# States beside heads: sums with the identity, 1/A moved to VectorE, six states of a batch added in pairs, and the first slot's order changed

## The chip, the cores and the metric

The kernel runs on one core of one Trainium2 chip. The metric is the device time of one execution in microseconds; the figure for a kernel is the median of its runs. Engines are named as in the profile: PE is TensorE (matrix products), PEld its weight loads, DVE is VectorE, ACT is ScalarE, POOL is GpSimd, SP the engine that issues most of the DMAs.

## What is computed

A decoder of three stages over 8 batches of 256 tokens with 128 features, all in float32. Stage one is a state-space block with 256 channels and 16 states, stage two a cross attention with 16 heads to a context of 256 tokens, stage three six layers of windowed attention and feed-forward. Each stage ends in a residual and a layer norm. The change lies in stages one and two. The state-space block, cut to what matters:

```python
X_main = silu(causal_conv4(Xn @ W_up1.T) + conv_b)          # [b, l, 256]
pp = X_main @ W_ll.T + b_ll
delta = softplus(pp[..., :256]); Bm = pp[..., 256:272]; Cm = pp[..., 272:]
A = -exp(A_log)                                              # [256, 16]
A_bar = exp(delta * A)
B_bar = (A_bar - 1) / (delta * A) * (delta * Bm)             # = (A_bar - 1) / A * Bm
H_t = A_bar_t * H_{t-1} + X_main_t * B_bar_t                 # a scan over 256 tokens
Y_t = sum over n of C_t[n] * H_t[:, n]
out = X + (Y * silu(Xn @ W_up2.T)) @ W_down.T + b_down
```

The factor 1/A belongs to a channel and a state and not to a time, so it can be applied before the scan or after it.

## The kernel before

**Tiles.** Channels lie on the partitions, as two halves `h` of 128; time (256) lies along the free axis, so a batch's work on one state is a tile of 128 x 512. Batches go in four pairs `p`; the convolution, the time steps `dt`, the gate and the B and C rows are made once a pair, for 512 tokens.

**Slots and steps.** The loop at the end of stage one calls `step(u, i)` for each batch u and state i (n in the code); k = 16u + i. The 16 steps of one batch are called slot u here. While slot u runs the states of batch u, batch u-1 goes through its cross attention: eight pairs of heads j = i - 6, in steps 6 to 13 and a little after. Slot 0 has no heads.

**Order.** A manual schedule holds PE, ACT, DVE and POOL to the order in which the program issues instructions, so what stands behind a waiting instruction on its engine waits too. Extra work is put into the steps by `at(u, i, when, ...)`, where `when` is E, M or L: early, in the middle or late in the step. A step runs in this order: the row fetch for k+4 (DMA on SP); `scores2` of head pair j (PE); `add_up` (PE); `denominators` (ACT) and `weight_sums` (POOL) of earlier heads; `scan(k)`; `outputs` (DVE); the E list; `decay_of(k+1)` (ACT); `clipped` (DVE, then ACT); `values2` (PE); the M list; `spread_b(k+2)`; the L list.

**One state.** `spread_b(k)` makes wz = x * B on DVE (L604, from `xm_ps` in PSUM and the row B; L608 for the first two states) and dw, its difference in time, on POOL (L613). `decay_of` makes ab = A_bar on ACT in a PSUM bank, two halves (recorded at L98); slots 1 to 7 have one bank for it, slot 0 two in turn. `scan` runs two scans on DVE (L631), m = (dw + m) * ab, and multiplies by the row C on POOL (mc, L633). `add_up` sums mc over the states in the PSUM bank `y`, as a matrix product per half whose weights are a diagonal of 1/A (`by_a`, L644); `decay` builds the 32 diagonals at the start on POOL (L408). `start_y` opens `y` with a product of 512 columns and the identity (L671). A float32 product runs as two passes, so the trace shows two matmuls, and two weight loads, for each in the code.

**Around it.** At the end of batch v's states `gated` (L676), `down` (L249, `dn_ps`) and `down_leave` (L254, `rr`) lead to the layer norm of v in steps 1 to 3 of the next slot: `ln_square` on ACT (L214), `ln_var` on PE (L218), `ln_roots` on ACT, `ln_latent` on DVE (L231, `la`). `queries` (L302, `q_ps`) and `queries_leave` follow in steps 4 to 11, `vals` (L287) and `keys` (L272) beside them. `prepare(p)` lays the making of pair p into the slots before it: statistics, `turn_x`, `copy_x` (L456), `norm_x`, `shifted` (L483), `conv` (L489, 16 passes of 512 columns into the two-bank tile `big`), `conv_tanh`, `conv_plus` (L504), `conv_out` (L508), `bc_product` and `bc_store` (L522, then by DMA to DRAM and back as rows), `gate_products` (L565), `dt_product` (L537) and `dt_parts`, `dt_log`, `dt_sum`. For p = 0 this is done ahead of slot 0, for p = 1 in slots 0 and 1, for p = 2 and 3 the convolution falls in slots 2 and 4 and `dt` in slots 3 and 5. `context_of(u)` norms and turns the context of batch u. `centre_rows` subtracts row means from `w_dn` and `wo` on ACT (L875).

## Time and profile before

| | us |
|---|---|
| median of 3 runs | 2152.8 (2150.98 to 2156.37) |
| profiled execution: its time / span from first to last instruction | 2151.4 / 2149.6 |
| first scan of slots 0 to 7 starts at | 31.8, 85.3, 149.8, 215.7, 282.7, 347.7, 413.8, 471.8 |
| yg of the last batch (end of the states) | 530.2 |
| busy, whole span: PE / DVE / POOL / ACT | 2035 / 1706 / 1649 / 1481 |

The slots take 53.5, 64.5, 65.9, 67.0, 65.0, 66.1, 58.0 and some 55 us; from about 546 us on the rest of the span is stage three, with PE busy in nine tenths and more of nearly every slice. A line of the profile names source line, engine, operation, the tiles out<-in, shape and count. A matmul's duration includes a tail that overlaps the next, so what a set of matmuls costs is read from start to start, or from the chain of waits, which counts only the time until the next link. Mean durations that matter here: L604 (wz, DVE, 128x512) 0.68 us, L613 (dw, POOL) 1.04, L633 (mc, POOL) 1.27, L631 (one half's scan, DVE) 0.67, ab (one half, ACT) 0.48, one pass of L644 (256 columns) 0.38 and of L671 (512 columns) 0.59.

### The profile page before, as it was taken

The numbers are of one execution on the slowest core, as the hardware profiler recorded it, in microseconds if no ns is written. First come the engines' busy times: TensorE is split into PE (matmuls) and PEld (weight loads), VectorE is DVE, ScalarE is ACT, GpSimd is POOL, SyncE is SP. The second block draws the span as 40 slices with busy tenths as digits, with TensorE's granted clock in tenths as the row PEclk, the third lists the DMA queues.
The fourth block names the chain that finished last, engine by engine and source line by source line (L and its number), as shares of the span: only waits on it lengthen the run. The fifth ranks groups of instructions, "written<-read, shape, count | busy, mean of one in ns | idle before, by whom it ended". The sixth has DMA issues, their size and how long they took to land.

```text
span 2149.6 us, 78066 instructions
## 1 busy us (share of the span) xinstructions
PE 2035.1 (95%) x32880; PEld 1376.6 (64%) x32880; DVE 1705.5 (79%) x2535; ACT 1481.2 (69%) x2657; POOL 1648.8 (77%) x1453
## 2 busy tenths in 40 slices
PE   6899999899989999999999999999999999999985
PEld 3555556566457776666766667676666767666663
DVE  5767767687589888888888888888888888888752
ACT  5767767666667777776676777677777767767654
POOL 4677767778599888888888888888888888888740
PEclk8999999999999999999999999999999999999997
DMA  4323323232244444343434344443443444333330
GB/s 120 94 63 71 62 68 73 64 74 65 79 74 70 71 95 72 70 77 68 92 71 78 69 75 86 74 78 66 88 74 70 78 71 82 66 66 66 61 57 10
DMA packets 455195, 156.13 MB, mean 73 GB/s; under 512 B 402046, under 2 KB 451068, under 8 KB 454716
## 3 DMA queue, kind: packets, MB, share of 16 engines
q1 hardware_dynamic: 454364, 150.76, 36.5%
q8 instruction: 258, 4.23, 0.9%
q14 instruction: 93, 0.76, 0.1%
q10 hardware_dynamic: 480, 0.38, 0.1%
HBM read 55.33 MB, written 1.31 MB: 26 GB/s over the span
## 4 chain that ended last, share of the span: by engine, by line
PE 77%; ACT 10%; DVE 10%; issue 2%; POOL 1%; DMA 0%; ACTq 0%; SPq 0%; DVEq 0%; POOLq 0%
PE qk_ps L1036 13%; PE y_ps L1213 8%; PE qkT_ps L1092 8%; PE o_ps L1199 7%; PE f_ps L1283 6%; PE v_ps L1036 6%; PE s_ps L1140 5%; PE pT_ps L1182 3%; PE f_ps L1311 3%; PE y L644 3%; PE o_ps L339 2%; PE s_ps L317 2%; DVE m L631 2%; DVE rb L1054 1%; PE k_ps L272 1%
## 5 line engine op out<-in xcount | busy, mean ns | idle before, releaser
L1057 POOL TENSOR_TENSOR qk<-qk,rb 128x512 f32<-128x512 f32 x384 | 481.3, 1276 | 53.3 <-DVE rb L1054 34.7
L1085 POOL TENSOR_TENSOR qk<-qk,rn 128x1024 f32<-128x1024 f32 x192 | 365.7, 1905 | 11.7 <-ACT rn L98 11.7
L1036 PE MATMUL qk_ps<-wqkv,xs 128*128 128x512 f32 x768 | 363.4, 595 | 1.6 <-ACT kz L1102 1.6
L1162 POOL TENSOR_TENSOR pw<-pw,mx 128x512 f32<-128x512 f32 x192 | 202.0, 1052 | 162.9 <-DVE mx L1161 162.6
L1059 ACT ACTIVATE sq<-qk_ps 128x1024 f32<-128x1024 f32 x192 | 197.0, 1026 | 168.2 <-PE o_ps L1199 120.8
L1053 DVE TENSOR_TENSOR qk<-qk_ps,tab 128x1024 f32<-128x1024 f32 x192 | 229.0, 1193 | 73.5 <-PE qk_ps L1036 71.9
L1054 DVE TENSOR_TENSOR rb<-qk_ps,tab 128x1024 f32<-128x1024 f32 x192 | 233.3, 1215 | 0.0
L1066 DVE TENSOR_REDUCE ss<-sq 128x16 f32<-128x1024 f32 x192 | 229.3, 1194 | 4.8 <-ACT sq L1059 4.8
L1175 POOL TENSOR_TENSOR pw<-pw,mx 128x512 f32<-128x512 f32 x192 | 200.6, 1045 | 39.0 <-ACT fxn L1270 32.0
L613 POOL TENSOR_TENSOR dw<-wz 128x512 f32<-128x512 f32 x128 | 133.2, 1041 | 111.2 <-DVE wz L604 97.4
L1213 PEld LDWEIGHTS y_ps<-oT,wo 128*128 128x128 f32 x1536 | 186.2, 192 | 46.7 <-issue 33.5
L1092 PE MATMUL qkT_ps<-ident,qk 128*128 128x128 f32 x1536 | 210.4, 279 | 4.0 <-POOL qk L1085 2.9
L1036 PEld LDWEIGHTS qk_ps<-wqkv,xs 128*128 128x128 f32 x768 | 131.5, 191 | 96.4 <-issue 93.5
L1207 DVE STREAM_TRANSPOSE oT<-o_ps 128x512 f32<-128x512 f32 x192 | 126.2, 696 | 80.6 <-PE o_ps L1199 80.6
L1213 PE MATMUL y_ps<-oT,wo 128*128 128x128 f32 x1536 | 187.5, 275 | 1.9 <-ACT pT L1186 1.6
L1140 PEld LDWEIGHTS s_ps<-kz,qT 64*32 64x32 f32 x12288 | 137.0, 105 | 74.4 <-issue 32.0
L633 POOL TENSOR_TENSOR mc<-m,rows 128x512 f32<-128x512 f32 x128 | 162.9, 1273 | 25.0 <-PE y L644 7.0
L1036 PE MATMUL v_ps<-wqkv,xs 128*128 128x512 f32 x384 | 180.8, 593 | 0.2 <-ACT sq L1059 0.2
L1092 PEld LDWEIGHTS qkT_ps<-ident,qk 128*128 128x128 f32 x1536 | 165.0, 141 | 24.4 <-POOL qk L1085 3.8
L1199 PE MATMUL o_ps<-vz,pT 64*32 64x64 f32 x12288 | 167.5, 225 | 0.7 <-issue 0.7
L631 DVE TENSOR_TENSOR_SCAN m<-dw,ab 128x256 f32<-128x256 f32 x256 | 160.7, 669 | 8.5 <-ACT ab L98 7.5
L98 ACT ACTIVATE pw<-pw 128x512 f32<-128x512 f32 x192 | 120.5, 628 | 66.9 <-POOL pw L1162 66.9
(210 smaller groups left out, 4117.3 us busy)
## 6 DMA issues: line engine op xcount, KB each, us to landing
vz<-v SPq DMA_DIRECT2D x1152, 64.0 KB, 2.2
rows<-bc_dram SPq DMA_DIRECT2D x128, 256.0 KB, 4.5
vz<-v SPq DMA_DIRECT2D x576, 32.0 KB, 2.6
wqkv<-in_L_ffn_Wqkv SPq DMA_DIRECT2D x18, 512.0 KB, 3.7
wo<-in_L_ffn_Wo SPq DMA_DIRECT2D x48, 64.0 KB, 3.2
w<-in_L_ffn_W SPq DMA_DIRECT2D x6, 341.0 KB, 3.8
t_in<-in_x SPq DMA_DIRECT2D x4, 256.0 KB, 3.6
wkv<-in_L_xattn_Wkv SPq DMA_DIRECT2D x1, 1024.0 KB
```

The costliest lines, as they stand in the source:

```text
L631: V.tensor_tensor_scan(m[:, t], dw[:, t], ab[:, t], 0.0, ALU.add, ALU.mult)
L1036: T.matmul(pr[:, i * 512 : (i + 1) * 512], lhsT=got[n]["xs"][:, tb * P : (tb + 1) * P], rhs=thirds[seq[n][0], c][:, i * 512 : (i + 1) * 51 ...
L1053: V.tensor_tensor(t, p3, cs, ALU.mult)
L1054: V.tensor_tensor(rb, p3, sn, ALU.mult)
L1057: G.tensor_tensor(t[:, :, o], t[:, :, o], rb[:, :, f], ALU.add)
L1066: V.tensor_reduce(got[n]["ss"][:, 2 * c + tb, :], got[n]["sq"], AX.X, ALU.add)
L1085: G.tensor_tensor(t, t, r, ALU.mult)
L1092: T.transpose(t_ps[:, hb * P : (hb + 1) * P], t[:, 2 * hb : 2 * hb + 2, :].rearrange("p h d -> p (h d)"), ident,)
L1140: T.matmul(s_ps[i * W : (i + 1) * W, e, c : c + 2 * W], lhsT=qT[r, 4 * g + i, j * W : (j + 1) * W], rhs=kz[r, 4 * g + i, k0 : k0 + 2 * W], ...
L1162: G.tensor_tensor(pw, pw, mx[:, 0].unsqueeze(3).to_broadcast([P, 4, 2, 2 * W]), ALU.subtract)
L1199: T.matmul(o_ps[i * W : (i + 1) * W, e, c : c + HD], lhsT=pT[r, j, i * W : (i + 1) * W], rhs=vz[r, j, i, :], start=True, stop=True, tile_p ...
L1213: T.matmul(y_ps[:, :P], lhsT=wts[d][0][:, hb, :], rhs=got[n]["oT", wh][:, hb // 4, (hb // 2) % 2, :].rearrange("p (w h q) -> p h w q", w=4 ...
```

## The change

- **Sums.** `by_a` and its 32 diagonals are gone. `add_up` adds a state with one product of 512 columns and the identity.
- **1/A.** `spread_b` multiplies by it: two `scalar_tensor_tensor` of 128x256 (one a half, x * 1/A * B) take the place of one product of 128x512.
- **Pairs.** In slots 1 to 7 the mc of states 0, 2 and 4 is held, POOL adds it to that of states 1, 3 and 5 (`pair_up`, at the end of the step), and one product sums both. 16 sums of a batch become 13; slot 0 keeps 16.
- **First slot.** `decay_of` runs two states ahead there. The convolution of pair 0 goes into two single banks. `cb`, `feed`, `start_y`, the gate, the preparation of pair 1 and the context's norm move to later steps; centring of `wo` moves to slot 1.
- **Other moves.** `queries` go from M to E and their copies from E of the next step to M, with the scale of q now in the copy (before: a product over wq in slot 0). `dt_product` goes from L to E with its followers a step earlier, `bc_product` from M to E. More buffers: rows 5 to 6, mc 5 to 7.

```diff
+PAIRED = (0, 2, 4)
...
-        A.copy(q.rearrange("p k t -> p (k t)"), st["q_ps"])
+        A.mul(q.rearrange("p k t -> p (k t)"), st["q_ps"], HD**-0.5)
...
-        by_a = wp.tile([P, 2, NS, P], FP, name="by_a")
...
-            for n in range(0, NS, 4):
-                for h in range(2):
-                    G.tensor_tensor(
-                        by_a[:, h, n : n + 4, :], ident.unsqueeze(1).to_broadcast([P, 4, P]),
-                        ia3[:, h, n : n + 4].unsqueeze(2).to_broadcast([P, 4, P]), ALU.mult,
-                    )
...
         def conv(p, c, h):
-            if not h:
-                c["acc"] = wide("conv")
+            if not p:
+                c["acc", h] = bank(("xm", "ab")[h], "conv")
+            elif not h:
+                t = wide("conv")
+                c["acc", 0], c["acc", 1] = t[:, :TP], t[:, TP:]
...
-                V.tensor_tensor(
-                    w[:, :, 1:], both(xms[u]), rows[k][:, 0:1, :].to_broadcast([P, 2, S]), ALU.mult
-                )
...
+            for h in range(2):
+                o = h * NS + n
+                if b_ps is None:
+                    x, r = both(xms[u])[:, h, :], rows[k][:, 0, :]
+                else:
+                    x, r = pairs[0]["xm"][:, h, :S], b_ps
+                V.scalar_tensor_tensor(w[:, h, 1:], x, ia[:, o : o + 1], r, ALU.mult, ALU.mult)
...
-            mc = sp.tile([P, TP], FP, name="mc", bufs=5)
+            mc = sp.tile([P, TP], FP, name="mc", bufs=7)
...
-            late.append((k, mc))
+            if k >= NS and k % NS in PAIRED:
+                held.append(mc)
+            else:
+                late.append((k, mc))
+
+        def pair_up(k):
+            if k >= NS and k % NS - 1 in PAIRED:
+                mc, k1 = held.pop(), late[-1]
+                G.tensor_tensor(k1[1], mc, k1[1], ALU.add)
...
-                for h in range(2):
-                    t = slice(h * S, (h + 1) * S)
-                    T.matmul(
-                        ys[u][:, t], lhsT=by_a[:, h, n, :], rhs=mc[:, t], start=False,
-                        stop=(n == NS - 1 and h == 1),
-                    )
+                T.matmul(ys[u], lhsT=ident, rhs=mc, start=False, stop=(n == NS - 1))
...
-                at(u, 2 * k + 4, "M", queries, st, k)
-                at(u, 2 * k + 5, "E", queries_leave, st, k)
+                at(u, 2 * k + 4, "E", queries, st, k)
+                at(u, 2 * k + 4, "M", queries_leave, st, k)
...
-                at(u, i, "L", dt_product, c, h)
-                at(u, i + 1, "L", dt_parts, c, h)
-                at(u, i + 2, "L", dt_log, c)
-                at(u, i + 3, "M", dt_sum, c, h)
+                at(u, i, "E", dt_product, c, h)
+                at(u, i, "L", dt_parts, c, h)
+                at(u, i + 1, "L", dt_log, c)
+                at(u, i + 2, "M", dt_sum, c, h)
...
-            decay_of(k + 1)
+            if u or i == NS - 1:
+                decay_of(k + 1)
+            elif i < NS - 2:
+                decay_of(k + 2)
...
-                if k:
-                    spread_b(k + 2)
-                else:
-                    spread_b(2)
+                spread_b(k + 2)
+            pair_up(k)
             beside(u, i, "L")
...
-        at(0, 1, "E", cb_product, c)
-        at(0, 1, "M", feed_product, 0)
-        at(0, 2, "M", feed, 0)
-        at(0, 2, "M", start_y, 0)
-        at(0, 2, "L", gate_products, 0, c)
-        at(0, 4, "E", gate_tanh, c)
-        at(0, 5, "E", gate_out, c)
...
+        at(0, 2, "M", cb_product, c)
+        at(0, 3, "E", feed_product, 0)
+        at(0, 4, "E", feed, 0)
+        at(0, 4, "E", start_y, 0)
+        at(0, 4, "M", gate_products, 0, c)
+        at(0, 6, "E", gate_tanh, c)
+        at(0, 7, "E", gate_out, c)
...
-        decay_of(0)
+        for k in range(2):
+            decay_of(k)
```

In `prepare(1)`, left out above, the convolution moves from steps 6 and 7 of slot 0 to 8 and 9, and all that follows it by two steps; in `context_of(0)` the root, norm and turn move from steps 7 to 13 to steps 13 and 14.

More of the change, by code (lines that the diff above doesn't have):

```diff
@@ L404, in decay @@
             V.reciprocal(ia, aa)
-            ia3 = ia.rearrange("p (h n) -> p h n", h=2)
-            for n in range(0, NS, 4):
-                for h in range(2):
-                    G.tensor_tensor(
-                        by_a[:, h, n : n + 4, :], ident.unsqueeze(1).to_broadcast([P, 4, P]),
-                        ia3[:, h, n : n + 4].unsqueeze(2).to_broadcast([P, 4, P]), ALU.mult,
-                    )
         def turn_decay():
@@ L485, in conv @@
         def conv(p, c, h):
-            if not h:
-                c["acc"] = wide("conv")
+            if not p:
[3 more added lines that the diff above has]
+                c["acc", 0], c["acc", 1] = t[:, :TP], t[:, TP:]
             for k in range(KC):
                 T.matmul(
-                    c["acc"][:, h * TP : (h + 1) * TP], lhsT=w_tap[:, h, k, :],
+                    c["acc", h], lhsT=w_tap[:, h, k, :],
                     rhs=xns[p % 2][:, :, k : k + S], start=(k == 0), stop=(k == KC - 1),
@@ L497, in conv_tanh @@
             with_table(
-                A.activation, c["xm"][:, h, :], c["acc"][:, h * TP : (h + 1) * TP], AF.Tanh,
+                A.activation, c["xm"][:, h, :], c["acc", h], AF.Tanh,
                 bias=half_b[:, h : h + 1],
@@ L508, in conv_out @@
             V.scalar_tensor_tensor(
-                m, c["acc"][:, h * TP : (h + 1) * TP], half_b[:, h : h + 1], m, ALU.add, ALU.mult
+                m, c["acc", h], half_b[:, h : h + 1], m, ALU.add, ALU.mult
             )
@@ L586, in fetch_rows @@
                 u, n = divmod(k, NS)
-                r = rows[k] = sp.tile([P, 2, S], FP, name="rows", bufs=5)
+                r = rows[k] = sp.tile([P, 2, S], FP, name="rows", bufs=6)
                 src = pairs[u // 2]["bc"].rearrange("(k n) t -> n k t", k=2)
@@ L591, in fetch_rows @@
                 )
-        rows, dws, abs_, late, ys, xms = {}, {}, {}, [], {}, {}
+        rows, dws, abs_, late, held, ys, xms = {}, {}, {}, [], [], {}, {}
         def both(t):
@@ L602, in spread_b @@
             wzs.append(w)
-            if b_ps is None:
-                V.tensor_tensor(
-                    w[:, :, 1:], both(xms[u]), rows[k][:, 0:1, :].to_broadcast([P, 2, S]), ALU.mult
-                )
-            else:
-                V.tensor_tensor(
-                    w[:, :, 1:], pairs[0]["xm"][:, :, :S], b_ps.unsqueeze(1).to_broadcast([P, 2, S]),
-                    ALU.mult,
-                )
+            for h in range(2):
[5 more added lines that the diff above has]
+                V.scalar_tensor_tensor(w[:, h, 1:], x, ia[:, o : o + 1], r, ALU.mult, ALU.mult)
             dws[k] = sp.tile([P, TP], FP, name="dw", bufs=3)
@@ L641, in add_up @@
                 u, n = divmod(k, NS)
-                for h in range(2):
-                    t = slice(h * S, (h + 1) * S)
-                    T.matmul(
-                        ys[u][:, t], lhsT=by_a[:, h, n, :], rhs=mc[:, t], start=False,
-                        stop=(n == NS - 1 and h == 1),
-                    )
+                T.matmul(ys[u], lhsT=ident, rhs=mc, start=False, stop=(n == NS - 1))
         def copy_xm(u):
@@ L741, in context_of @@
             at(u, 5, "L", ctx_stats, st)
-            at(u, 7, "L", ctx_root, st)
-            at(u, 9, "L", ctx_norm, st)
-            at(u, 12, "M", ctx_turn, st)
-            at(u, 13, "E", ctx_leave, st)
+            at(u, 7 if u else 13, "L" if u else "E", ctx_root, st)
+            at(u, 9 if u else 13, "L", ctx_norm, st)
+            at(u, 12 if u else 14, "M" if u else "E", ctx_turn, st)
+            at(u, 13 if u else 14, "E", ctx_leave, st)
             at(u, 14, "M", keys, st, 0)
@@ L779, in prepare @@
                 at(u, 2, "L", x_stats, c, False, range(2, 4))
-                at(u, 3, "E", x_roots, c)
+                at(u, 3, "M", x_roots, c)
                 at(u, 3, "L", load_table, "exp_and_others")
-                at(u, 4, "M", centre_x, c, range(4))
-                at(u, 4, "L", turn_x, c)
-                at(u, 5, "L", norm_x_after, c)
-                at(u, 6, "E", turn_x, c)
-                at(u, 6, "L", shifted, p, c)
-                t = 6
+                at(u, 4, "L", centre_x, c, range(4))
+                at(u, 5, "M", turn_x, c)
+                at(u, 6, "L", copy_x, c)
+                at(u, 7, "E", norm_x, c, range(4))
+                at(u, 7, "M", turn_x, c)
+                at(u, 8, "E", shifted, p, c)
+                t = 8
             at(u, t, "L", conv, p, c, 0)
@@ L797, in prepare @@
             at(u, t + 4, "L", load_table)
-            at(u, t + 5, "M", bc_product, c)
-            at(u, t + 6, "E", bc_store, c)
+            at(u, t + 5, "E", bc_product, c)
+            at(u, t + 5, "L", bc_store, c)
             at(u, 23, "L", cb_product, c)
@@ L839, in step @@
             if k + 2 < B * NS:
-                if k:
-                    spread_b(k + 2)
-                else:
-                    spread_b(2)
+                spread_b(k + 2)
+            pair_up(k)
             beside(u, i, "L")
@@ L882, in decoder_kernel @@
         at(0, 0, "L", load2)
-        at(0, 1, "E", cb_product, c)
-        at(0, 1, "M", feed_product, 0)
-        at(0, 2, "M", feed, 0)
-        at(0, 2, "M", start_y, 0)
-        at(0, 2, "L", gate_products, 0, c)
-        at(0, 4, "E", gate_tanh, c)
-        at(0, 5, "E", gate_out, c)
-        at(0, 10, "L", centre_out)
-        at(0, 12, "L", lambda: A.mul(w2["wq"], w2["wq"], HD**-0.5))
+        at(0, 2, "M", cb_product, c)
[5 more added lines that the diff above has]
+        at(0, 7, "E", gate_out, c)
+        at(0, 10, "M", centre_out)
         for k in range(0, NHB, 2):
-            at(0, 12 + k // 2, "L", lambda k=k: centre_rows(w2["wo"], w2["wo_m"], range(k, k + 2)))
+            at(1, 10 + k // 2, "L", lambda k=k: centre_rows(w2["wo"], w2["wo_m"], range(k, k + 2)))
         with_table(A.activation, aa, cols[:, _OFF["a_log"] : _OFF["a_log"] + 2 * NS], AF.Exp)
@@ L947, in decoder_kernel @@
         at(0, 1, "E", copy_x, c)
-        at(0, 6, "M", centre_rows, w_dn, dn_m, range(2))
+        at(0, 8, "L", centre_rows, w_dn, dn_m, range(2))
         for u in range(B):
```

## The prediction

> **What bounds the kernel now.** First the busy table of the page, then the busy time by stage, then inside a stage the chain of waits, then the instructions in order of time. The change touches only stages one and two, up to 546 us of 2149.6; the other 1604 us are attention and feed-forward layers that it leaves alone. So I ask which engine ends each slot (16 states of one batch) and how late it is.

> By stage (columns: stretch, length, PE, weight loads, DVE, ACT, POOL busy, PE clock, DMA share, GB/s), for slots 0, 4 and 6:

> ```profile
> 31.80:85.30 53.50, 39.50 (x122) 24.38 (x123) 37.70 (x78) 35.23 (x73) 37.80 (x34) 0.81 0.40 90
> 282.70:347.70 65.00, 63.10 (x316) 39.03 (x315) 48.38 (x81) 44.34 (x85) 46.44 (x40) 1.00 0.32 69
> 413.80:471.80 58.00, 55.13 (x296) 35.36 (x295) 47.23 (x79) 39.12 (x79) 46.36 (x40) 1.00 0.37 76
> ```

> Slot 4 is TensorE's: 63.1 of 65.0. Slot 0 is nobody's: no engine above 39.5 of 53.5, so waits set it. Slot 6 has 2.9 us of TensorE idle. The chain of waits in slot 4 shows what one sum of a state costs (start, length, engine, tile, line):

> ```profile
> 287.67 0.86 PE y L671 x2
> 288.52 0.86 PE y L644 x4
> ...
> 308.43 1.06 PE y L644 x4
> ```

> Two passes of 512 columns with the identity (L671) take 0.86, four of 256 (L644) take 0.86 as well: **columns are paid, not instructions**. After the 64-row score products the set costs 1.06, the switch of tile form included. Slot 6 in order of time, where states 0 to 3 meet the layer norm:

> ```profile
> 419.47 1.03 PE L644 MATMUL y<-mc,by_a 128*128 128x256 f32 x4
> 420.33 1.03 PE L249 MATMUL dn_ps<-yg,w_dn 128*128 128x256 f32 x4
> 421.39 0.42 DVE L254 TENSOR_TENSOR rr<-dn_ps,x 128x256 f32<-128x256 f32 x1 [2.10 <-PE dn_ps L249]
> 421.74 0.68 DVE L604 TENSOR_TENSOR wz<-xm_ps,rows 128x512 f32<-128x512 f32 x1
> 422.05 1.03 PE L644 MATMUL y<-mc,by_a 128*128 128x256 f32 x4
> 422.56 1.04 POOL L613 TENSOR_TENSOR dw<-wz 128x512 f32<-128x512 f32 x1 [3.34 <-DVE wz L604]
> 422.92 1.02 PE L218 MATMUL ln_var<-ln_sq,mean_w 128*128 128x512 f32 x2
> ```

> The sum at 422.05 is that of state 1 and stands ahead of the variance product in TensorE's order; the dw of state 3 ends at 423.60.

> **Sums over 512 columns.** 26 sums instead of 32 halves in slots 1 to 7, and no price per column changes. For a sum that stays I take 0; bounds 0 and -0.2 (1.06 less 0.86, if the exposed switch shrank). What is saved is three sums a slot, 21 x 0.86 = 18.1 us of TensorE, worth something only where TensorE is late.

> [...]

> **1/A in VectorE's product.** L604's one product of 128x512 (0.68, next start 0.60 later) becomes two of 128x256 with a column scalar. Nearest rows of that form: L231 at 471 ns, L265 at 480. Two make 0.94, less the usual overlap of 0.08 each: 0.78. So **+0.18 us a state** on DVE. Bounds: +0 and +0.8 (two at the 747 ns of L508, a 128x512 form). Beside heads DVE holds scan 1.18, oT 0.34, w 1.13 and this 0.78 = 3.43 a step against TensorE's 1.06 + 1.06 + 1.44 = 3.56: just hidden. In the early steps of slots 6 and 7 it hides behind ACT's ab (0.98), for which the next scan waits anyway. Without the cover it would be 112 x 0.18 = 20 us.

> The eight L408 products that vanish (8.03 us of POOL from 9.64) were hidden: POOL then idles 13.0 us for wz.

> **Pairs on GpSimd.** Three adds of 128x512 a slot, at the 1.27 of L560, the same plain add of two tiles: 3.8 us of POOL, which has 11.6 us idle in slot 6. The price is in the order. pair_up(k) stands on POOL behind dw(k+2), which waits for wz(k+2); and step k+1 opens with the sum that needs it, at the head of TensorE's queue. **Step 2**, slot 6: TensorE skips state 0, so rr and wz come 0.86 earlier; wz is 0.18 longer; dw ends at 423.60 - 0.68 = 422.92; the pair at 424.15; its sum at 425.05. The variance product behind it starts at 425.05, not 422.92: **+2.1**. Behind that wait ACT's roots and then ab(4), behind ab scan(4); on DVE la, wz(5), scan(4). Slots 5, 6, 7 alike: 6.4. In slots 1 and 3 the turn of x and ACT's norm behind it are late instead: +1.5 and +1.0. In slots 2 and 4 the convolution (3.44) stands ahead and hides it: 0. **Step 4**: dw(5) is again followed by the pair (1.25), the sum (0.9), then q_ps(0), v_ps and their copies on ACT, ab(6) queued behind: in slot 6 q_ps moves from 428.41 to 433.5, ab(6) from 431.54 to 435.85, that is 2 beyond the first delay. Slots 6, 7: 1.9 each; 5: 1.6; 1: 1.2; 3: 1.4; 2, 4: 0.1: together 8.2. **Step 6**: in slots 2 and 4 wz(7) stands behind the convolution's output on DVE, dw(7) ends at 309.2, the pair at 310.4, and the sum moves from 308.43 to 310.4 where TensorE is the bound: +2.0 each; slots 6, 7: +0.6: together 5.2. **Sum of the waits +22.3**; bounds 0 (TensorE late everywhere) and 30 (a third more, if the layer norm's other products queue too).

> **Moved products.** q and dt products now stand ahead of o_ps, where TensorE idles 0.7 to 1.0 in step 8 for oT (o_ps waits 14.2 us in slots 1 to 7). In slot 3 I moved them by hand: the d_ps of 1.72 at 249.1 goes into the idle of 0.97, ACT's ez and z come a step earlier, and the last o_ps moves from 276.07 to 273.8: -2.3. Slots 1, 3, 5: -6.9; 6, 7: -0.7 each; total **-8.3**, bounds 0 and -11.4 (3.8 of idle each). The rows of wo, 4 x 0.68 of ACT, go from slot 0 to slot 1's steps 10 to 13, beside a chain that runs through ACT: **+1.5**, bounds 0 and 2.7. The scale of wq (1.04) goes into copies that run anyway: 0.

> **Start and slot 0.** tanh of the first half starts at 17.04, after both convolutions, though ACT is free at 12.2; with two tiles it can start after the first (9.89 + 3.5). The second then is the only one behind: bc at 19.2, not 21.39. Of these 2.2 us, ab(1) ahead of iaT and the longer wz take 0.9: scan(0) at 30.5, not 31.77. Through the 16 steps in the new order (scan 1.18, wz 0.78, ab 0.95 two ahead, mc 1.22, dw 1.0) the waits left are: cb at 37.8, s_ps at half clock until 41.2, g_ps and five saved sums until 51, so that copy_x and ab(9) hold scan(9) 2.6 us; the convolutions until 63, so that conv_out holds DVE 3.2 us; keys and xs at the end. scan(16) falls at 80.2, not 85.30: **-5.1** in all, bounds -10 (a further 4.9 if the two holds and half the end vanish) and +1 (below).

> The clock in slot 0 is 0.5 from 32.5 to 46.1 and a set of s_ps takes 2.08 there, 1.07 later; later convolutions behind a thin TensorE could meet it: 2 x 3.45 more at worst, of which ab's lead hides about 1, hence the +1. [...]

> SP issues the same row loads, with a sixth buffer; c0's load comes half a step earlier. No queue gets more.

> **Sum.** -5.1 + 22.3 - 8.3 + 1.5 = +10.4 by hand schedule. A delay in one place is often partly taken back by an idle gap later (slot 6 has 2.9 us), so I take 2 off: +8. The profiled execution took 2151.4 (span 2149.6, 1.8 around it), 1.4 under the median of 2152.8; differences carry over: 2152.8 + 8 = **2161**.

> **Rivals.** *The waits cancel the gain of slot 0*: half the waits (11) are found; 2152.8 - 5.1 + 11 - 8.3 + 1.5 = 2152. For it: ACT and DVE have idle gaps later in each slot. Against: those of step 6 lie where TensorE never catches up. *The wait never shows* (the other side, faster): the pair is done before TensorE arrives at steps 2, 4 and 6 because it is late by more than about 3 us everywhere. Then -5.1 - 8.3 + 1.5, and 2 x 2.6 of sums in slots 2 and 4: 2136. Against: slot 6 has y waiting for mc already (1.11 at 425.05), so TensorE isn't late there. *Sums really get cheaper*: 0.2 each on 107 sums, 21 us: 2161 - 21 = 2140. *VectorE becomes the bound*: at +0.8 a state the step beside heads is 4.05 against 3.56, 56 x 0.5 = 28: 2189; it decides from +0.31 a state on (3.56 less the 3.25 of today), and the nearest rows put it at 0.18.

> **Chances.** Forecast (2155 to 2170) 0.57, cancelling 0.14, no wait 0.17, cheaper sums 0.06, VectorE 0.06. About 0.3% (6.5 us) can be told from no change: faster is no wait, cheaper sums and a tail of cancelling, 0.24; same is the rest of cancelling and the foot of the forecast, 0.20; slower is the forecast's body and VectorE, 0.56. Range 2137 to 2170, the forecast's own 2155 to 2170.

> **What would show it.** Right: in slots 5 to 7 y waits for POOL 2 to 3 us in step 2 and ln_var follows it; scan(16) near 80; y at 0.86. Wrong: no such wait; y under 0.8 for a state; wz pairs above 0.9 with scans waiting for DVE; scan(16) outside 75 to 86.

## The result and the profile after

The changed kernel takes **2182.6 us** (median of 4 runs, 2182.0 to 2187.5) against 2152.9 (4 runs) of the kernel before beside it: ratio 1.0141, 95% interval 1.0122 to 1.0161. It is slower by some 30 us where 8 were forecast, and outside the range of 2137 to 2170.

The first scans of slots 0 to 7 and the last yg tell where. In the profiled executions (after: 2182.3, span 2180.5):

| | start | slot 0 | 1 | 2 | 3 | 4 | 5 | 6 | 7 | from yg on |
|---|---|---|---|---|---|---|---|---|---|---|
| before | 31.8 | 53.5 | 64.5 | 65.9 | 67.0 | 65.0 | 66.1 | 58.1 | 58.4 | 1619.3 |
| after | 30.8 | 51.3 | 71.0 | 70.1 | 68.0 | 69.5 | 69.0 | 63.2 | 65.0 | 1622.5 |

Start and slot 0 give 3.2 back, slots 1 to 7 lose 30.9, and the part whose code is the same loses 3.2. (Slot 7 before takes 58.4 us up to the last yg; the "some 55" given with the times before is too short.)

By stage, slots 0, 4 and 6 of the kernel after (columns as shown for before; the eighth figure is the granted clock of PE):

```profile
30.80:82.10 51.30, 36.18 (x92) 16.95 (x92) 42.64 (x95) 29.85 (x62) 37.08 (x33) 0.82 0.48 92
291.20:360.70 69.50, 63.35 (x278) 33.14 (x277) 51.86 (x97) 44.53 (x85) 49.76 (x43) 0.95 0.31 65
429.70:492.90 63.20, 54.29 (x258) 29.43 (x257) 49.72 (x95) 39.05 (x79) 49.74 (x43) 0.95 0.36 69
```

Slot 4 was TensorE's by 63.1 of 65.0; now it is busy 63.35 of 69.5, so its idle time has grown from 1.9 to 6.15 us. And the clock, 1.00 in both slots before, is 0.95. Slot 6 in order of time (start, length, engine, line, and in brackets the idle time before, with what ended it):

```profile
437.60 1.04 POOL L607 TENSOR_TENSOR dw<-wz 128x512 f32<-128x512 f32 x1 [2.52 <-DVE wz L605]
438.60 1.27 POOL L638 TENSOR_TENSOR mc<-mc 128x512 f32<-128x512 f32 x1
...
439.93 1.12 PE L644 MATMUL y<-mc,ident 128*128 128x512 f32 x2 [2.85 <-POOL mc L638]
...
440.89 1.02 PE L219 MATMUL ln_var<-ln_sq,mean_w 128*128 128x512 f32 x2
...
446.63 1.27 POOL L638 TENSOR_TENSOR mc<-mc 128x512 f32<-128x512 f32 x1
...
447.95 2.07 PE L644 MATMUL y<-mc,ident 128*128 128x512 f32 x2 [5.18 <-POOL mc L638]
...
449.81 1.91 PE L303 MATMUL q_ps<-la,wq 128*128 128x256 f32 x4
...
454.49 1.26 DVE L625 TENSOR_TENSOR_SCAN m<-dw,ab 128x256 f32<-128x256 f32 x2 [3.66 <-ACT ab L99]
```

Step 2 is as forecast: dw, then the pair of 1.27, then the sum that had TensorE waiting, then the variance product. Step 4 has the same chain, but look at the lengths: the sum takes 2.07 and q_ps 1.91, where at full clock they take 1.02 to 1.13 and 1.03. The profile grants the clock 0.5 from 445.4 to 452.2. **After the wait TensorE runs at half clock**, and the scan behind q_ps and ab comes later still. The chain of waits in slot 4 (start, length to the next link) shows the plain, the waiting and the half-clock sum:

```profile
302.06 0.86 PE y L644 x2
...
309.82 1.12 PE y L644 x2
...
319.08 2.07 PE y L644 x2
```

What PE waited for between 82 and 560 us (total, times, longest), after:

```profile
PE y L644 <- POOL mc L638: 42.4, 16, 5.2
PE o_ps L340 <- DVE oT L359: 10.1, 18, 1.4
```

The wait for the pair is by far the first. Within slots 1 to 7 the clock is at half for nine stretches of 3.4 or 6.8 us, 47.8 us in all, with TensorE busy 38.7 of them; before, for none.

### The profile page after: what moved, and what is told of

The parts are those of the page before. It is cut to its first block, busy times and chain, and to the rows that moved or that the text cites. A ratio compares the mean times of both kernels' runs of the same rounds, so it can differ in the third digit from the quotient of the medians.

```text
span 2180.5 us, 77544 instructions
## 1 busy us (share of the span) xinstructions
PE 2034.3 (93%) x32582; PEld 1330.5 (61%) x32582; DVE 1728.4 (79%) x2663; ACT 1479.0 (68%) x2654; POOL 1665.0 (76%) x1466
## 4 chain that ended last, share of the span: by engine, by line
PE 75%; DVE 10%; ACT 10%; issue 2%; POOL 2%; DMA 0%; ACTq 0%; POOLq 0%; DVEq 0%
PE qk_ps L1035 13%; PE y_ps L1212 8%; PE qkT_ps L1091 8%; PE o_ps L1198 7%; PE f_ps L1282 6%; PE v_ps L1035 6%; PE s_ps L1139 5%; PE pT_ps L1181 3%; PE y L644 3%; PE f_ps L1310 3%; PE o_ps L340 2%; PE s_ps L318 1%; DVE m L625 1%; DVE rb L1053 1%; PE k_ps L273 1%
## 5 line engine op out<-in xcount | busy, mean ns | idle before, releaser
L1174 POOL TENSOR_TENSOR pw<-pw,mx 128x512 f32<-128x512 f32 x192 | 200.7, 1046 | 39.5 <-ACT fxn L1269 32.0
L625 DVE TENSOR_TENSOR_SCAN m<-dw,ab 128x256 f32<-128x256 f32 x256 | 160.4, 667 | 18.7 <-ACT ab L99 18.1
L1151 DVE TENSOR_TENSOR pw<-s_ps,mask 128x512 f32<-128x512 f32 x192 | 123.4, 684 | 54.0 <-PE s_ps L1139 54.0
```

Of the source, the lines that this page charges most:

```text
L1174: G.tensor_tensor(pw, pw, mx[:, 1].unsqueeze(3).to_broadcast([P, 4, 2, 2 * W]), ALU.mult)
```

## The experiments

Theory W: the order of the pair (POOL makes it after dw, TensorE stands before it) costs a wait, and the wait costs the clock. Rival V: VectorE's two products. Rival S: the work dealt anew. A kernel's loss is given in medians, and by slots from its profiled execution, where single runs scatter less: in kernels with the same code there, the start alone moves by 2 us (first scan at 30.8 to 33.1) and the part from yg on lies between 1614.5 (the kernel without pairs) and 1623.0.

**No pairs.**

```diff
-PAIRED = (0, 2, 4)
+PAIRED = ()
```

> The changed kernel with no state paired, everything else kept. Theory W (TensorE stands waiting for GpSimd's pair at the head of its queue, and after each such wait runs some 3.4 to 7 us at half clock): both are gone, 2140 to 2155, and between the first scan of slot 1 and the last yg TensorE's granted clock never falls to half. Rival V (the two products with a column scalar in VectorE, 0.87 us a pair against 0.60 to 0.68 before, make the loss): 2175 to 2185, as with the pairs. Rival S (slots 1 to 7 lose by the work dealt anew, q, dt and the rows of wo): 2175 to 2185 too.

Measured 2140.2 (2137.8 to 2144.3), ratio to before 0.9955 (0.9940 to 0.9971): 42.4 under the changed kernel (40 by the two ratios), and **under the kernel before too**. Its slots 4 and 6:

```profile
277.00:341.50 64.50, 62.60 (x284) 33.17 (x283) 50.82 (x97) 44.24 (x85) 46.39 (x40) 1.00 0.31 70
...
405.30:463.30 58.00, 55.12 (x264) 29.39 (x263) 49.60 (x95) 39.02 (x79) 46.35 (x40) 1.00 0.39 75
```

The clock is 1.00 again, TensorE is busy 62.6 of 64.5, and slots 1 to 7 take 439.2 against 475.8 after and 444.9 before. V and S fall as causes of the loss: everything but the pairs is still in this kernel.

**The sum a step later**, and **the pair ahead of dw**. Pairs as in the change in both; in the first, TensorE's product of a pair is put off by one step, in the second GpSimd's order is turned round.

```diff
-        def add_up():
+        def add_up(now=10**6):
             while late and late[0][0] // NS in ys:
+                k = late[0][0]
+                if k >= NS and k % NS - 1 in PAIRED and now < k + 2:
+                    break
                 k, mc = late.pop(0)
...
-            add_up()
+            add_up(k)
```

```diff
+            pair_up(k)
             if k + 2 < B * NS:
                 spread_b(k + 2)
-            pair_up(k)
```

> The changed kernel, but TensorE takes a paired sum one step later than it does, so that the pair has a whole step to be made in; the pairs themselves, and so the three sums saved a slot, are kept. Theory W: the waits of y for the pair fall from 3 us to under 0.5 each, half clock is gone from slots 1 to 7, 2130 to 2150, at or under the kernel without pairs by up to 10 us. Rivals V and S: 2175 to 2185. A fourth possibility, that GpSimd's three adds of 1.27 a slot themselves delay mc and dw: 5 to 15 us above the kernel without pairs.

> The changed kernel with GpSimd's pair issued ahead of dw(k+2) instead of behind it; the pair then no longer stands behind VectorE's product for state k+2, and dw(k+2) is 1.3 us later where GpSimd has no gap. Theory W: the pair is ready some 2 us earlier in most places, the waits of y fall from 3 us to about 1 and half clock appears in few places, 2150 to 2168. Rivals V and S: 2178 to 2190, as the dw are later and nothing else changes.

Later: 2138.6, ratio 0.9942 (0.9927 to 0.9957). First: 2146.2, ratio 0.9978 (0.9967 to 0.9989). PE's waits for the pair, in the kernel with the later sum and then in the kernel with the pair first:

```profile
PE y L647 <- POOL mc L638: 4.2, 3, 1.4
```

```profile
PE y L644 <- POOL mc L638: 19.8, 10, 3.6
```

From 42.4 after to 19.8 and 4.2, and the time follows. Not all came as expected: the pair ahead of dw is faster than the 2150 to 2168 written down, and with the later sum three waits of up to 1.4 and 6.8 us of half clock remain in slots 1 to 7, where none was expected. The pair itself is nearly free; its place is what costs. But 21 saved sums of 0.86 (18.1 us) are worth little even with so little wait left: 1.6 us in medians and 5.1 in slots 1 to 7 (434.1 against 439.2). Slots 2 and 4, where TensorE is the bound, gain 2.4 each, the full price of three sums (2.6); slots 1, 3 and 5 gain 0.1 to 0.8, and slots 6 and 7 lose 1.1 and 0.3.

**Extra products in the wait.** Products of zeros ahead of each paired sum, first four, then two; they add nothing to y.

```diff
+    zero = keep.tile([P, TP], FP, name="zero")
+    G.memset(zero, 0.0)
...
+                if u and n - 1 in PAIRED:
+                    for _ in range(4):
+                        T.matmul(ys[u], lhsT=ident, rhs=zero, start=False, stop=False)
                 T.matmul(ys[u], lhsT=ident, rhs=mc, start=False, stop=(n == NS - 1))
```

> The changed kernel with four extra products of 512 columns of zeros ahead of every paired sum (they add zero to y), 1.7 us of TensorE at full clock; they stand where TensorE waits for the pair, so that it is busy for part of the wait. Theory W in its second half (the idle stretch lowers the clock, and the low clock costs time of its own): half clock is gone from most of slots 1 to 7 and the time falls by 5 to 18 us, 2164 to 2178. If the wait alone costs and the low clock is hidden: 2180 to 2190, the extra products costing what does not fit into the waits (21 x 1.7 = 36 us at most).

> The changed kernel with two extra products of zeros ahead of every paired sum, where the run before had four. One of 512 columns is two passes and costs 0.86, not 0.43, so four took 3.6 us, longer than the wait of 3 us; two take 1.7 and fit into it. If the low clock costs time of its own: half clock leaves slots 1 to 7 and the time falls to 2162 to 2177. If it does not: 2179 to 2187, where the run with four was as well.

Four: 2186.2, in the range written down for "the wait alone costs". But the expectation had the price wrong by half: a float32 product is two passes, so four took 3.6 and outlasted the wait; this run could not decide. Two: **2175.5**, 7 under the changed kernel (5.6 by the two ratios, whose intervals overlap; 6.5 in slots 1 to 7, 469.3 against 475.8), with 6.8 us of half clock in slots 1 to 7 instead of 47.8. It is a gain by making TensorE do more, as the low clock's own price would have it. It is also a lower bound: in step 2 of slots 2 and 4, where there was no wait, the extra products cost 1.7 each.

**One part of the change alone:** the kernel before with VectorE's two products and the sums with the identity, nothing else:

```diff
...
-                V.tensor_tensor(
-                    w[:, :, 1:], both(xms[u]), rows[k][:, 0:1, :].to_broadcast([P, 2, S]), ALU.mult
-                )
...
+                V.scalar_tensor_tensor(w[:, h, 1:], x, ia[:, o : o + 1], r, ALU.mult, ALU.mult)
...
-                    T.matmul(
-                        ys[u][:, t], lhsT=by_a[:, h, n, :], rhs=mc[:, t], start=False,
-                        stop=(n == NS - 1 and h == 1),
-                    )
+                T.matmul(ys[u], lhsT=ident, rhs=mc, start=False, stop=(n == NS - 1))
...
```

> The kernel before with one part of the change alone: 1/A as a column scalar in VectorE's product (two of 256 columns a state) and the sums over 512 columns with the identity; no pairs, first slot and orders as before. As predicted (a kept sum costs the same 0.86, and the longer product hides beside heads): 2147 to 2156, the slots 1 to 7 within 2 us of before. Rival V (the product's extra 0.2 us a state shows): 2160 to 2175. Rival C (the sums get cheaper, because half the loads are gone): 2130 to 2144.

Measured 2153.5 (12 runs), ratio 1.0011 (1.0002 to 1.0020). Slots 1 to 7, in the kernel before and then in this one:

```profile
85.30:530.20 444.90, 416.69 (x2135) 260.10 (x2134) 336.87 (x559) 314.49 (x614) 333.61 (x288) 1.00 0.31 69
```

```profile
87.70:535.70 448.00, 417.19 (x1910) 217.24 (x1909) 355.55 (x670) 314.38 (x614) 337.39 (x292) 1.00 0.34 66
```

225 passes and as many recorded weight loads fewer, and TensorE is busy 0.5 us longer: columns are paid. VectorE is busy 18.7 more (0.17 for each of 112 states) and slots 1 to 7 are 3.1 longer, where at most 2 were expected. V and the rival of cheaper sums both fall.

**The moves put back** (no pairs; q, dt and bc products of slots 1 to 7 in their old places):

```diff
-                at(u, 2 * k + 4, "E", queries, st, k)
-                at(u, 2 * k + 4, "M", queries_leave, st, k)
+                at(u, 2 * k + 4, "M", queries, st, k)
+                at(u, 2 * k + 5, "E", queries_leave, st, k)
...
-            at(u, t + 5, "E", bc_product, c)
...
+            at(u, t + 5, "M" if p > 1 else "E", bc_product, c)
...
-                at(u, i, "E", dt_product, c, h)
...
+                at(u, i, "L", dt_product, c, h)
...
```

> The changed kernel without pairs (it ran at 2140), and with the q, dt and bc products of slots 1 to 7 put back into the places they had before. If the moves are worth the 8.3 us that were predicted for them: 2146 to 2151. If they are worth nothing: 2138 to 2142. The slots 1 to 7 of the kernel without pairs took 439.2 from first scan to last yg against 444.9 before, so some 4 to 6 us are the likeliest, 2144 to 2147.

Measured 2152.8 (12 runs), 12.6 over the kernel without pairs: **the moves are worth more than any expectation had**. Slots 1 to 3 of this kernel:

```profile
83.90:151.90 68.00, 59.15 (x265) 28.94 (x264) 51.18 (x95) 51.85 (x109) 49.33 (x43) 0.97 0.32 72
151.90:218.00 66.10, 63.96 (x287) 33.60 (x286) 52.81 (x106) 44.98 (x86) 47.05 (x41) 1.00 0.37 67
218.00:285.30 67.30, 61.06 (x281) 31.70 (x280) 51.64 (x98) 50.40 (x101) 49.28 (x43) 1.00 0.27 64
```

Without pairs and with the moves the seven slots take 64.6, 65.3, 64.7, 64.5, 63.8, 58.0 and 58.2; with the moves undone 68.0, 66.0, 67.3, 65.2, 66.4, 58.9 and 59.0. The differences are 3.4, 0.7, 2.6, 0.7, 2.6, 0.9 and 0.8, 11.8 in all. Slots 2 to 7 are those of the kernel with VectorE's part alone to 0.1; slot 1 is 3.0 longer (68.0 against 65.0), with the rows of wo the one thing that is added there. Part of these 3.0 can be the clock's: behind the added rows TensorE waits 2.6 us for oT, and a stretch of 3.4 us at half clock follows (from 143.2 on), which the kernel with the moves doesn't have. If the moves are worth in slot 1 the 2.6 of slots 3 and 5, they make 11.0 in all and the rows cost 2.2 beside them.

**Pairs beside the heads** (states 6 to 11, summed a step later):

```diff
-PAIRED = (0, 2, 4)
+PAIRED = (6, 8, 10)
```

> The kernel whose paired sums are taken a step later (it ran at 2139), with the pairs moved from states 0 to 5 to states 6 to 11, beside the heads, where TensorE is busy 3.5 of every 3.6 us. If TensorE's columns are the bound there, the three sums saved a slot, 21 x 0.86 = 18 us, are nearly all found: 2122 to 2130. If GpSimd's add (1.27 beside mc 1.27 and dw 1.04 a step of 3.6) makes mc or dw late, or VectorE's chain is as long as TensorE's: 2137 to 2146.

Measured 2154.7, 14.5 over no pairs: a miss, though both outcomes were named. PE's waits in this kernel:

```profile
PE o_ps L340 <- DVE oT L359: 19.8, 29, 1.7
PE o_ps L346 <- POOL ws L332: 12.2, 19, 1.1
```

The second line is new: GpSimd also makes `ws`, the sum of the weights of a head pair, 1.27. With mc 1.27 and dw 1.04 it holds 3.58 of a step of 3.6. The expectation had left ws out; there was no room for an add. By slots it costs 1.8 to 2.1 each in slots 2, 4, 6 and 7 and 0.1 to 0.3 in the others, 8.7 in all. The two profiled executions lie 19.0 apart; 8.5 of that is behind yg and 1.8 ahead of slot 1, where the code is the same.

**Each pair alone.** The order as changed, with `PAIRED` as (0,), (2,) or (4,).

> The changed kernel with the first pair alone (states 0 and 1, summed in step 2), against the kernel without pairs at 2140. The prediction's price for step 2 is 8.8 us: 2149. What the two traces show at the scan of step 4, slots 1 to 7 together, is 10.7: 2151. With the two rivals so near, the slots tell: +3.2, -0.9, +1.4, -0.9, +3.3, +1.5, +3.1 if the low clock that followed this wait in slots 1, 5 and 7 costs 1.7 each; +1.5, 0, +1.0, 0, +2.1, +2.1, +2.1 by the prediction.

> The changed kernel with the second pair alone (states 2 and 3, summed in step 4), against 2140. The prediction's price for step 4 is 8.2: 2148. The two traces show 17.1 between the scans of steps 4 and 6, mostly in slots 1, 6 and 7 (3.2, 3.8, 3.8): 2157 if the three pairs add up independently. If step 4 costs so much only because the pair of step 2 has come before (y waited 5.2 there in slots 6 and 7, and 2.9 in step 2): 2146 to 2151.

> The changed kernel with the third pair alone (states 4 and 5, summed in step 6), against 2140. The prediction's price for step 6 is 5.2, all but 1.2 of it in slots 2 and 4 (+2.0 each): 2145. The two traces show 8.9, +4.3 in slot 2 and +4.8 in slot 4 and nothing elsewhere, with TensorE at half clock for 6.8 us behind the wait in both: 2149. If the half clock needs the earlier pairs' idle time too: slots 2 and 4 at +2 to +3, 2143 to 2146.

| alone | median | over no pairs | by slots 1 to 7 (profile) | sum | half clock in slots 1 to 7 |
|---|---|---|---|---|---|
| step 2 | 2154.0 | 13.8 | 2.4, -0.9, 1.3, -0.9, 2.8, 1.5, 2.7 | 8.9 | 13.7 |
| step 4 | 2164.9 | 24.7 | 3.2, 1.2, 4.6, 1.2, 4.5, 4.3, 3.9 | 23.0 | 30.7 |
| step 6 | 2161.0 | 20.8 | 2.2, 5.1, 2.5, 5.5, 2.4, 2.6, 0.9 | 21.0 | 27.3 |

All three medians lie above every value that was written down for them. In step 2 the slots have the expected pattern, with 0.1 to 0.8 less in those at half clock. (The profiled execution of this kernel is the fastest of its ten, 2149.1, that of step 6 the slowest of its five, 2167.4; the slots belong to these.) Steps 4 and 6 cost more alone than in company, and the three sum to 52.9 where the change loses 36.6: they don't add. Step 6 in slots 1, 3 and 5 costs 2.2 to 2.5 alone, with half clock behind it, and nothing in the change. Why the wait is shorter there once two earlier ones have passed wasn't settled. Slot 4 with the third pair alone:

```profile
316.39 2.07 PE L644 MATMUL y<-mc,ident 128*128 128x512 f32 x2 [2.05 <-POOL mc L638]
...
318.26 1.91 PE L303 MATMUL q_ps<-la,wq 128*128 128x256 f32 x4
...
320.10 2.53 PE L511 MATMUL bc_ps<-xm,w_ll 128*32 128x512 f32 x4
...
323.75 1.23 DVE L326 TENSOR_SCALAR w<-s_ps 128x1024 f32<-128x1024 f32 x1 [4.77 <-PE s_ps L318]
```

Two sets of products at nearly double length and a third, bc_ps, at 2.53 where it takes 1.90 at full clock; VectorE waits 4.8 for the scores behind them: a wait of 2.05 has grown to a loss of 5.5.

**The clock by itself.** The first pair alone, with two products of zeros ahead of its sum in slots 1, 3, 5, 6 and 7.

```diff
+                if u in (1, 3, 5, 6, 7) and n == 1:
+                    for _ in range(2):
+                        T.matmul(ys[u], lhsT=ident, rhs=zero, start=False, stop=False)
```

> The first pair alone, with two products of zeros (0.86 each, 1.7 in all) ahead of its sum in slots 1, 3, 5, 6 and 7, where the sum waits 2.85 or more; none in slots 2 and 4. They lie inside the wait and end before the pair does, so the wait is as long as with the first pair alone and only the clock differs. If the low clock has a price of its own: no half clock in slots 1 to 7 and every one of these slots at +1.4 to +1.6 over the kernel without pairs, some 5 us less in all than the first pair alone. If the wait is all: the same time as the first pair alone, within 2 us.

Measured 2149.6 against 2154.0 for the first pair alone, with no half clock in slots 1 to 7; by slots 1.8, -0.9, 1.1, -0.9, 1.5, 1.5, 1.5, so slots 1 and 3 miss the expected 1.4 to 1.6 by 0.2 and 0.3. Slot 5 without the extra products, and with them:

```profile
354.18 1.58 PE L644 MATMUL y<-mc,ident 128*128 128x512 f32 x2 [2.85 <-POOL mc L638]
...
355.55 1.91 PE L219 MATMUL ln_var<-ln_sq,mean_w 128*128 128x512 f32 x2
...
357.50 0.45 ACT L99 ACTIVATE ln_root<-ln_var,tiny 128x256 f32<-128x256 f32 x1 [3.60 <-PE ln_var L219]
```

```profile
350.51 1.02 PE L648 MATMUL y<-zero,ident 128*128 128x512 f32 x2
...
352.66 1.13 PE L649 MATMUL y<-mc,ident 128*128 128x512 f32 x2 [1.14 <-POOL mc L640]
353.63 1.02 PE L221 MATMUL ln_var<-ln_sq,mean_w 128*128 128x512 f32 x2
...
354.69 0.45 ACT L101 ACTIVATE ln_root<-ln_var,tiny 128x256 f32<-128x256 f32 x1 [2.29 <-PE ln_var L221]
```

In both kernels the sum starts 1.3 after the pair does, on the same wait; from its start to that of ACT's root it is 3.32 us without and 2.03 with the extra products. The 1.3 stay: slot 5 loses 2.8 in one, 1.5 in the other, slot 7 2.7 and 1.5, and slot 6, which met no half clock in either, 1.5 in both. **The low clock has a price of its own**, shown here for step 2: 3.2 us in four slots, where some 5 were expected.

**A better version.** No pairs (0.9955, 0.9940 to 0.9971) and pairs summed a step later (0.9942, 0.9927 to 0.9957) beat both kernels. They can't be told apart, and the one without pairs is the simpler.

## Why the prediction was wrong

Against the profiled executions (+30.9), step by step:

- **Sums over 512 columns, 0:** right. They stay at 0.86 in the chain, and the part alone changes TensorE's busy time by 0.5. (The prediction's 26 are passes: a batch goes from 32 products of 256 columns, 64 passes, to 13 of 512.)
- **1/A in VectorE, hidden:** right within 3 us. 0.17 a state was paid, as the 0.18 said; 3.1 of 18.7 us shows.
- **Moved products, -8.3:** right in mechanism and place (slots 1, 3, 5: -3.4, -2.6, -2.6 against -2.3 each), mis-sized: -11.8, just past the bound of -11.4. **Rows of wo, +1.5:** +3.0, past the bound of 2.7. (If the moves are worth 2.6 in slot 1 as well, they are -11.0 and the rows +2.2, both inside their bounds.) Together with VectorE's 3.1 that makes -5.7 in slots 1 to 7 against -6.8.
- **Start and slot 0, -5.1:** -3.2; scan(16) at 82.1, inside the 75 to 86, not at 80.2. Where the 1.9 went was not tried.
- **The waits for the pair, +22.3, less 2 for recovery:** this is the step that failed. It priced the wait and put the half clock behind it at nothing. The mechanism of the wait was there, mostly in the named places; the size was +36.6 in slots 1 to 7:

| | slot 1 | 2 | 3 | 4 | 5 | 6 | 7 | sum |
|---|---|---|---|---|---|---|---|---|
| step 2 predicted | 1.5 | 0 | 1.0 | 0 | 2.1 | 2.1 | 2.1 | 8.8 |
| measured | **3.2** | -0.9 | **1.4** | -0.9 | **3.3** | 1.5 | **3.1** | 10.7 |
| step 4 predicted | 1.2 | 0.1 | 1.4 | 0.1 | 1.6 | 1.9 | 1.9 | 8.2 |
| measured | **3.2** | 1.2 | 2.0 | 1.2 | 1.9 | **3.8** | **3.8** | 17.1 |
| step 6 predicted | 0 | 2.0 | 0 | 2.0 | 0 | 0.6 | 0.6 | 5.2 |
| measured | 0 | **4.3** | -0.1 | **4.8** | 0 | -0.1 | -0.1 | 8.8 |

Measured is the scans of steps 4, 6 and 8 of the changed kernel against those of the kernel without pairs. Bold are the nine places with half clock behind the wait. There the measured exceeds the predicted by 1.7, 0.4, 1.2, 1.0, 2.0, 1.9, 1.9, 2.3 and 2.8, together 15.2; in the twelve other places by -0.8 in sum. So **the waits were sized well in sum, and what they do to TensorE's clock was left out.** Single places miss by up to 1.1 either way (step 4 in slots 2 and 4: 1.2 where 0.1 was predicted; step 2 there: -0.9, the sum saved, where 0 was). The prediction had the clock in view, as a bound of 1 us in slot 0, and did not carry it to the waits it had just worked out. In slot 0 of the kernel before, TensorE was busy for 0.94 of the 3.41 us ahead of the half clock at 32.5.

That the excess is the clock's can be read from the kernel with two extra products, place by place. In the nine bold places it loses 1.8, 1.1, 1.5, 1.5 (step 2), 1.6, 3.1, 3.3 (step 4), 1.9 and 3.2 (step 6): 19.1 together against 31.0 in the changed kernel and 15.7 predicted. So 11.9 of the 15.2 go with the half clock, although the extra products lengthen TensorE's work. Of the 3.4 that stay, 2.6 are in step 4 of slots 6 and 7, the only two places where this kernel still meets half clock; another 1.2 in step 6 of slot 4 has none behind it. In the other places of step 4 the two kernels agree to 0.01 us. For step 2 the run with the first pair alone shows the same.

- **Less 2 for recovery:** wrong. Step by step, what a slot had lost at step 8 it had still lost at its end, to 0.2.
- **From yg on, 0:** +3.2, with the same code. That part varies by 8.5 between kernels that leave it alone. It goes with the clock there too: of the fourteen profiles the five shortest such parts (1614.5 to 1616.4) hold 23 to 37 us at half clock, the nine others (1618.7 to 1623.0) 37 to 48. No run tests it, so the cause stays open.

Of the signs named, those for the forecast were all seen (y waits 2.85 in slots 5 to 7, ln_var follows, y at 0.86, scan(16) at 82.1 where "near 80" was named) and none of those against it: the list had no sign for the clock. The rival at 2189 lay nearer in number, but its mechanism is refuted: VectorE's part alone takes 2153.5.

## What to carry to other kernels

An add moved to an engine that has room for it cost here by its place in two queues, not by its length: adds of 1.27 in the same steps cost 42.4 us over no pairs in the order as changed, 6.0 ahead of dw, and nothing that can be told with the sum a step later (beside the heads GpSimd had no room, 3.58 of 3.6 us being taken, and there they cost 14.5). So put the consumer a step later, or the add ahead of what it needn't follow, before counting what it saves. Whoever forecasts a new wait on TensorE should price the work behind it at half clock too, and look where the wait leaves it little to do in a stretch of 3.4 us (in these runs half clock followed all 31 of the stretches counted below in which it was busy for 0.42 or less at full clock). And a product taken from an engine is worth its time only in the stages which that engine ends: 2.4 of 2.6 us here in slots 2 and 4, nothing in slots 6 and 7.

## What the runs showed of the hardware

```profile
351.30:354.71 3.41, 0.56 (x2) 0.30 (x2) 3.41 (x8) 1.25 (x3) 2.85 (x3) 1.00 0.18 52
354.71:358.12 3.41, 3.41 (x6) 1.35 (x5) 0.71 (x2) 0.59 (x2) 2.85 (x3) 0.50 0.22 46
416.16:419.57 3.41, 1.77 (x7) 0.84 (x5) 2.46 (x6) 0.68 (x2) 1.10 (x2) 1.00 0.44 94
419.57:422.98 3.41, 2.20 (x5) 1.06 (x6) 2.46 (x5) 1.09 (x3) 3.41 (x4) 1.00 0.03 11
```

TensorE was busy for 0.16 of the first stretch, and the next was at half clock; it was busy for 0.52 and 0.64 of the two in slot 6, and the clock stayed full.
